# Summing, norming and projecting the tokens of layer 3 inside its first block of queries

## The chip, the core and the metric

The kernel runs on one core of a Trainium2 chip. The core has a matrix engine (TensorE, "PE" in the profile; its weight loads are listed as "PEld"), a vector engine (VectorE, "DVE"), an engine for activation functions (ScalarE, "ACT"), a general engine (GpSimd, "POOL") and a queue for transfers (SyncE, "SP"). Each engine works through its own instructions in order and waits for others by semaphores. Working memory is SBUF, matrix products land in PSUM (eight banks), and everything larger is in DRAM, which transfers (DMA) read and write.

The metric is the time of one execution on the device in microseconds, as a median over several runs; lower is better.

## The reference

A network of four layers on an image of 256 channels and 64 x 64 points, in float32. Layers 0 and 1 work on the image, layers 2 and 3 on its 4096 points as tokens of 256 numbers. Layers 2 and 3 each add an attention to the tokens and then a mixture of eight experts, of which each token uses two. The change lies between the experts of layer 2 and the attention of layer 3:

```python
t = t + _L2_ffn_ref(_ln_t(t), ...)                 # experts of layer 2
t = t + _L3_attn_ref(_ln_t(t), Wq, bq, Wk, bk, Wv, bv)
t = t + _L3_ffn_ref(_ln_t(t), Wg, bg, W1, b1, W2, b2)

def _L3_attn_ref(x, Wq, bq, Wk, bk, Wv, bv):
    Q = x @ Wq + bq; K = x @ Wk + bk; V = x @ Wv + bv
    weights = softmax(Q @ K.T / sqrt(256))         # 4096 x 4096
    return weights @ V
```

`_ln_t` takes each token's mean away and divides by its deviation.

## The kernel before, in words

**Names.** A token tile is 128 tokens (there are 32), a block is four tiles, 512 tokens (eight blocks, `NBLK`, index `b`), a pair is two tiles (16 pairs, `NPAIR`, index `j`). The tokens stay in SBUF as `t`.

**Layer 2's experts** (`experts`, L1844; `expert_tiles`, L1861) read sorted tokens from the DRAM table `xs` and write each token's two outputs to the DRAM table `ys` with scattered transfers (L1925). The table is filled by scatters of layer 2's route (L1784). Between the two, `attn3` has begun: it forms the product of the weights of queries and keys (`wqk`, L2033 to L2037) and the weights of values (`wvp`, L2028) from three matrices that are loaded under the name `weights3` (L2335, L2336). Tiles are allotted from pools that are stacked: a pool opened later lies behind those still open, and a tile that lies in memory of an earlier pool waits until the earlier tile is done with.

**Norm and projection** (L2043 to L2068, called "the stage between" in this document). For each of the eight blocks: `combine` loads the experts' two outputs (`f_g`, 512 KB each, one half issued on SP's queue, one on ScalarE's) and adds them to `t` with two additions on VectorE (L1963). `layer_norm` (L192) takes statistics on VectorE, the root on ScalarE (L204), and applies the norm on ScalarE (L211); the result is written into `vs`, the tile of values. TensorE turns it (L2052), ScalarE copies it to `ks` (L2054), TensorE multiplies it with `wqk` (L146 through `mm`), ScalarE adds the bias (L2060), and the queries go to DRAM (`qd`, L2061). VectorE forms four sums and differences of keys (L2063 to L2066), and the keys go to DRAM (`kd`, L2068). `ks` has two buffers.

**The attention** (L2069 on). All products are made by a scheme with seven products in place of eight on halves of the matrices, which needs sums and differences of the operands. It goes over blocks of queries and within each over pairs of keys; one (block, pair) is a step `g`, 128 steps in all.

- `fetch(g)` (L2086) loads the keys of a pair (`kt`), with the first pair of a block also the queries, of which VectorE makes four differences (L2093 to L2096). In the first block it also takes a maximum over the keys (L2104) and forms four sums and differences of values in place on GpSimd (L2107 to L2110).
- `scores(g)` (L2122) is seven products into three PSUM banks. One bank (`sa`) is written, copied by ScalarE (L2132), added to by VectorE (L2133), and written again within the step. `together` (L2112) combines them with four operations on VectorE, ScalarE takes exponentials (L2144), and VectorE forms their differences `et` with three operations (L2147 to L2149).
- `values(g)` (L2152) is seven products of exponentials with values, summed in four PSUM banks over the pairs of a block.
- `finish` (L2172) multiplies with `wvp`, divides by the sum and adds to `t`, for one tile of the block before; `route` (L1730) norms those tokens, picks the experts and scatters them to `xs`. Its tile of norms `rn` and its turned tile `rT` have one buffer each.

In the loop (L2186) `values` follows `scores` by `LAG` = 1 step. Within `manual_schedule` TensorE's instructions stand in the order in which they are written; on the other engines and queues a planner sets the order, from its own estimate of when each instruction can start, with what is written earlier going first among those that can.

Of the kernel before, what the change touches and what calls it, by code (L numbers as in the profile page):

```python
# [19 lines left out]
P = 128  # L20
# [33 lines left out]
LAG = 1  # L54
# [34 lines left out]
class Net:  # L89
# [1071 lines left out]
    def store(self, t, out, more=False):  # L1161

        with (
# [3 lines left out]
            for b in range(NBLK):  # L1167
                o = pool.tile([P, 2, NB], F32, tag="o", name="st_o")
                y = self.outputs(b, pool) if more else None
# [779 lines left out]
    def outputs(self, b, pool):  # L1949

        y = pool.tile([P, 2, TPB, C], F32, tag="g", name="f_g")
# [5 lines left out]
    def combine(self, b, t, pool):  # L1957

        nc = self.nc
        y = self.outputs(b, pool)  # L1960
        part = t[:, b * TPB : (b + 1) * TPB, :]
        for r in range(2):
            nc.vector.tensor_tensor(part, part, y[:, r], ALU.add)  # L1963
# [43 lines left out]
    def attn3(self, t, S):  # L2007
# [6 lines left out]
        with (  # L2014
# [12 lines left out]
            wvp = w["w_v3p"]  # L2027
            nc.vector.tensor_tensor(wvp, wvp, w["w_v3s"], ALU.subtract)  # L2028
            with tc.tile_pool(name="a3m_ps", bufs=1, space=PSUM) as ps:
# [9 lines left out]
            with (  # L2039
                tc.tile_pool(name="a3n", bufs=2) as wp,  # L2040
                tc.tile_pool(name="a3n_ps", bufs=2, space=PSUM) as ps,
            ):
                for b in range(NBLK):  # L2043
                    self.combine(b, t, wp)
                    n = [vs[:, 2 * b + i // 2, 2 * (i % 2) : 2 * (i % 2) + 2, :].rearrange("p s c -> p (s c)") for i in range(TPB)]
                    self.layer_norm(wp, t[:, b * TPB : (b + 1) * TPB, :], n, 1e-5, on_act=True)

                    ks = wp.tile([P, 2, 8, P], F32, tag="ks", name="a3_ks")
                    for k in range(2):
                        p = ps.tile([P, NB], F32, tag="tr", name="tr_ps")  # L2050
                        for i in range(TPB):
                            nc.tensor.matmul(p[:, i * P : (i + 1) * P], n[i][:, k * P : (k + 1) * P], self.ident, is_transpose=True,  # L2052
                                             start=(i == 0), stop=(i == TPB - 1))
                        nc.scalar.copy(ks[:, :, 2 * k : 2 * k + 2, :], p.rearrange("p (r s n) -> p r s n", r=2, s=2))  # L2054
                    nc.vector.memset(vs[:, 2 * b : 2 * b + 2, 1 : 4 : 2, P - 1 : P], 1.0)
                    qT = wp.tile([P, 2, NB], F32, tag="qT", name="a3_qT")
                    for m in range(2):
# [408 lines left out]
```

## Time and profile before

| what | us |
|---|---|
| median of 5 runs (3776.49 to 3793.88) | 3778.69 |
| the profiled execution | 3789.68 |
| its span, first to last instruction | 3787.8 |
| last scatter of layer 2's experts issued (L1925) | 2256.2 |
| first load of experts' outputs issued (L1954) | 2259.2 |
| first turn (L2052) on TensorE | 2276.1 |
| last projection done on ScalarE (L2060) | 2328.7 |
| first product of scores (L2128) | 2337.1 |
| first product of the second block of queries | 2437.2 |
| last product of values, about | 3171.8 |
| first load of tokens for layer 3's experts (L1875) | 3206.6 |

Over the span TensorE is busy 90%, VectorE 58%, GpSimd 38%, ScalarE 36%. Times inside the execution are counted from the span's start. A row of the order of time gives start, length, engine, line, operation, what is written and read, and in brackets the idle time before it with what ended it. A row of a group gives busy time in all and the mean time of one in ns after the first bar, and the idle time before after the second. TensorE's rows count two instructions for one product in float32.

### The profile page before, as it was taken

The page shows a single profiled execution, that of the slowest core. Times are in us where ns is not written, and L with a number is a line of the kernel's source. Part 1 is how long each engine was busy: PE and PEld are TensorE (multiplying, and loading weights), DVE is VectorE, ACT ScalarE, POOL GpSimd, SP SyncE. Part 2 cuts the span into 40 slices and gives each one's busy share as a digit, 9 for nine tenths or more (in the row PEclk, how much of TensorE's full clock was granted, in tenths as well). Part 3 has the DMA queues.
Part 4 walks back from the last instruction along what each step waited for, and adds up shares of the span by engine and source line. Part 5 has one row for each costly group of instructions (what it writes and reads, how often), then busy time and mean ns, then how long its engine had stood idle before and what let it go on. Part 6 is the DMA issues. An engine that isn't in the chain of part 4 may idle for free. (4 is left out here: it accounts for less than half of the span.)

```text
span 3787.8 us, 59679 instructions
## 1 busy us (share of the span) xinstructions
PE 3415.9 (90%) x22332; PEld 2393.8 (63%) x22332; DVE 2210.8 (58%) x5433; ACT 1360.3 (36%) x2783; POOL 1433.6 (38%) x1416
## 2 busy tenths in 40 slices
PE   6989999999997788986876977999999996999997
PEld 4433334334333688854665754888888885888886
DVE  6756656566565577788554547777777775111111
ACT  5544343343432566432111334222222221333331
POOL 1038888888883455534323333000000001111110
PEclk9999999999998899998785998999999997999999
DMA  1004414301013322200001866232232322555554
GB/s 56 3 28 114 130 56 122 101 24 40 21 40 127 94 68 68 68 18 1 24 33 52 271 216 240 89 101 85 94 100 96 96 95 88 196 200 186 195 189 175
DMA packets 160975, 378.27 MB, mean 100 GB/s; under 512 B 17377, under 2 KB 75490, under 8 KB 151458
## 3 DMA queue, kind: packets, MB, share of 16 engines
q1 hardware_dynamic: 136450, 318.96, 25.7%
q0 software_dynamic: 13056, 35.93, 2.5%
q10 hardware_dynamic: 11168, 19.42, 1.5%
q8 instruction: 182, 2.98, 0.3%
q14 instruction: 119, 0.97, 0.1%
HBM read 273.96 MB, written 100.29 MB: 99 GB/s over the span
## 5 line engine op out<-in xcount | busy, mean ns | idle before, releaser
L583 POOL TENSOR_TENSOR l_sm<-l_sc,mask 128x512 f32<-128x512 f32 (+3 forms) x624 | 770.0, 1270 | 118.8 <-ACT l_sc L573 116.4
L577 DVE TENSOR_TENSOR l_sm<-l_s,mask 128x256 f32<-128x256 f32 (+3 forms) x1248 | 492.1, 447 | 300.6 <-PE l_s L567 290.9
L573 ACT COPY l_sc<-l_s 128x384 f32<-128x384 f32 (+3 forms) x896 | 367.6, 461 | 558.2 <-PE l_s L567 541.4
L567 PE MATMUL l_s<-l_q,l_k 32*128 32x384 f32 (+2 forms) x3584 | 425.6, 515 | 5.6 <-DVE l_sm L577 2.4
L146 PE MATMUL f_h_ps<-f_xT,f_w 128*128 128x256 f32 x1440 | 346.6, 389 | 16.2 <-DVE f_xT L1888 6.5
L1784 POOL DMA_INDIRECT xs<-f_n,f_to x64 | 62.7, 980 | 788.4 <-DVE a_qt L2096 577.1
L1925 POOL DMA_INDIRECT ys<-f_y,f_at x144 | 138.9, 965 | 577.9 <-ACT f_y L1924 530.4
L146 PE MATMUL f_y_ps<-f_w,f_h 128*128 128x256 f32 x1440 | 328.1, 379 | 0.0
L146 PEld LDWEIGHTS f_h_ps<-f_xT,f_w 128*128 128x128 f32 x1440 | 266.4, 192 | 85.8 <-ACT f_h L1898 20.9
L567 PEld LDWEIGHTS l_s<-l_q,l_k 32*128 32x128 f32 x3584 | 165.6, 184 | 241.4 <-issue 125.2
L146 PEld LDWEIGHTS f_y_ps<-f_w,f_h 128*128 128x128 f32 x1440 | 268.2, 190 | 33.7
L2144 ACT ACTIVATE a_e<-a_e 128x512 f32<-128x512 f32 x256 | 156.8, 629 | 241.9 <-DVE a_e L2117 222.8
L952 DVE TENSOR_TENSOR l_pr<-l_vk,l_w_ps 128x1280 f32<-128x1280 f32 x128 | 186.5, 1481 | 55.1 <-PE l_acc_ps L956 37.5
L1898 ACT ACTIVATE f_h<-f_h_ps,f_w 128x256 f32<-128x256 f32 x360 | 163.7, 468 | 134.3 <-PE f_h_ps L146 125.3
L956 PE MATMUL l_acc_ps<-ident,l_pr 128*128 128x128 f32 x1600 | 196.9, 277 | 9.3 <-POOL l_pr L947 9.2
L956 PEld LDWEIGHTS l_acc_ps<-ident,l_pr 128*128 128x128 f32 x1600 | 183.5, 143 | 15.8 <-POOL l_pr L947 10.9
L1924 ACT ACTIVATE f_y<-f_y,f_wgt 128x256 f32<-128x256 f32 x144 | 65.3, 500 | 329.8 <-DVE f_y L1922 296.9
L610 PE MATMUL l_a_ps<-l_sm,l_v 128*32 128x512 f32 (+3 forms) x1408 | 178.7, 530 | 1.9 <-POOL l_sm L583 1.8
L610 PE MATMUL l_b_ps<-l_sm,l_v 128*32 128x256 f32 (+2 forms) x2176 | 171.5, 376 | 0.5 <-POOL l_sm L583 0.5
L2128 PE MATMUL a_sa_ps<-a_q,a_kt 128*128 128x256 f32 x512 | 155.7, 386 | 17.9 <-DMA a_kt<-a_kd 9.1
L2132 ACT COPY a_u<-a_sa_ps 128x256 f32<-128x256 f32 x128 | 47.6, 372 | 328.3 <-PE a_sa_ps L2128 314.6
L1922 DVE TENSOR_TENSOR f_y<-f_y_ps,f_w 128x512 f32<-128x512 f32 x72 | 49.8, 691 | 196.2 <-PE f_y_ps L146 188.5
(500 smaller groups left out, 6318.4 us busy)
## 6 DMA issues: line engine op xcount, KB each, us to landing
a_kt<-a_kd SPq DMA_DIRECT2D x128, 512.0 KB
f_w<-in_f_w SPq DMA_DIRECT2D x36, 1152.0 KB
f_w<-in_f_w SPq DMA_DIRECT2D x36, 1028.0 KB
xs<-zero SPq DMA_DIRECT2D x8, 4160.0 KB
l_vk<-vt SPq DMA_DIRECT2D x180, 128.0 KB
f_x<-xs SPq DMA_DIRECT2D x72, 260.0 KB
f_w<-in_f_w SPq DMA_DIRECT2D x36, 384.0 KB
l_rcp<-l_recd SPq DMA_DIRECT2D x48, 256.0 KB
```

The lines of the kernel that those rows point to most:

```text
L146: self.nc.tensor.matmul(out, lhsT, rhs, start=(i == 0), stop=(i == len(pairs) - 1))
L567: nc.tensor.matmul(s[pair, j], k[hp, key * P : (key + 1) * P], qs[hp], start=True, stop=True)
L573: nc.scalar.copy(sc[:, j], s[1, j])
L577: nc.vector.tensor_tensor(sms[0][:, j, at : at + t * wide].rearrange("p (t n) -> p t n", n=wide), part[:, which, :], mask, ALU.mult)
L583: nc.gpsimd.tensor_tensor(sms[1][:, :, at : at + t * wide].rearrange("p j (t n) -> p j t n", n=wide), part[:, :, which, :], bc(mask, 1, 2) ...
L610: nc.tensor.matmul(out, v[:, key, hp], sms[pair][:, j, base + lo * wide : base + hi * wide], start=not seen[nm], stop=(left[nm] == 0 and h ...
L952: nc.vector.tensor_tensor(pr, vk, bc(held["w"][:, j, dy], 3, D), ALU.mult)
L956: nc.tensor.matmul(acc[:, m, j, :], pf[:, dx, m * P : (m + 1) * P], self.ident, is_transpose=True, start=(j == 0 and dy == 0 and dx == 0 a ...
L1898: nc.scalar.activation(h[:, m, :], q, AF.Gelu, bias=w1[:, 2 * hidden + m : 2 * hidden + m + 1])
L1925: nc.gpsimd.indirect_dma_start(out=self.ys_parts[(i % 4) * NI + k], in_=y[:, k, :], in_offset=None, out_offset=bass.IndirectOffsetOnAxis(a ...
L2128: mm = lambda out, i, right: nc.tensor.matmul(out, A[i], right, start=True, stop=True)
L2144: nc.scalar.activation(e[:, i : i + 3 : 2], e[:, i : i + 3 : 2], AF.Exp, scale=1.0 / 16.0)
```

## The change

The stage between is taken apart into three functions, `norm(b)` (load, sum, norm), `turn(b, k)` (one half of the turn and its copy) and `ask(b, m)` (one half of the projection; with the second half also the writes of queries and keys and the differences of keys). Blocks 0 and 1 are done ahead of the loop. Blocks 2 to 7 are done in steps 0 to 11 of the first block of queries: in an even step the turn, in an odd step the projection, one half between `scores` and `values`, one half after them; `norm` is written one block ahead. `LAG` becomes 2. In the first block of queries `et` is formed on GpSimd, and GpSimd's order, too, is as written. `fetch(g + 3)` is written at the end of a step and no longer at its start.

Memory: the loaded sums, the route's norms and its turned tile share one tile, `room`, with two buffers; `ks` has one buffer; the queries share a tile with the attention's output. `wvp` gets a tile of its own in the pool `a3`, and the pool `weights3` is opened inside `attn3`, behind the pool `a3`, and closed before the experts of layer 2 begin.

```diff
-LAG = 1
+LAG = 2
...
-            wvp = w["w_v3p"]
-            nc.vector.tensor_tensor(wvp, wvp, w["w_v3s"], ALU.subtract)
-            with tc.tile_pool(name="a3m_ps", bufs=1, space=PSUM) as ps:
+            wvp = pool.tile([P, 2, C + 1], F32, tag="wvp", name="a3_wvp")
+            with (
+                tc.tile_pool(name="weights3", bufs=1) as wpool,
+                tc.tile_pool(name="a3m_ps", bufs=1, space=PSUM) as ps,
+            ):
+                self.weights(wpool, ["w_qkT3", "w_v3p", "w_v3s"])
+                nc.vector.tensor_tensor(wvp, w["w_v3p"], w["w_v3s"], ALU.subtract)
...
+                banks = ["q", "sa", "sb", "sc"]
+                kss, qTs = {}, {}
...
+                room = lambda: wp.tile([P, TPB * CX + 2 * NB], F32, tag="room", name="f_room")
+
+                def norm(b):
+
+                    y = room()[:, : 2 * TPB * C].rearrange("p (r i c) -> p r i c", r=2, c=C)
+                    self.outputs(b, y)
+                    part = t[:, b * TPB : (b + 1) * TPB, :]
+                    for r in range(2):
+                        nc.vector.tensor_tensor(part, part, y[:, r], ALU.add)
+                    self.layer_norm(wp, part, [places(b, i) for i in range(TPB)], 1e-5, on_act=True)
...
+                def turn(b, k):
+
+                    if k == 0:
+                        kss[b] = wp.tile([P, 2, 8, P], F32, tag="ks", name="a3_ks", bufs=1)
+                    p = bank()
+                    for i in range(TPB):
+                        nc.tensor.matmul(p[:, i * P : (i + 1) * P], places(b, i)[:, k * P : (k + 1) * P], self.ident, is_transpose=True,
+                                         start=(i == 0), stop=(i == TPB - 1))
+                    nc.scalar.copy(kss[b][:, :, 2 * k : 2 * k + 2, :], p.rearrange("p (r s n) -> p r s n", r=2, s=2))
+
+                def ask(b, m):
+
+                    ks = kss[b]
+                    if m == 0:
+                        nc.vector.memset(vs[:, 2 * b : 2 * b + 2, 1 : 4 : 2, P - 1 : P], 1.0)
+                        qTs[b] = wp.tile([P, 2, NB], F32, tag="oT", name="a3_qT", bufs=1)
+                    p = bank()
+                    self.mm(p, [(wqk[:, kt, m * P : (m + 1) * P], ks[:, :, 2 * kt : 2 * kt + 2, :]) for kt in range(2)])
+                    nc.scalar.activation(qTs[b][:, m, :], p, AF.Identity, bias=bqk[:, m : m + 1])
+                    if m == 1:
+                        nc.sync.dma_start(out=qd[b], in_=qTs[b])
...
                 def route(t0, T):
-                    rn = wp.tile([P, TPB, CX], F32, tag="rn", name="f_n", bufs=1)
-                    rT = wp.tile([P, 2, NB], F32, tag="rT", name="f_nT", bufs=1)
-                    return self.route(t0, T, t, S, wp, rn[:, :T], rT[:, :, : T * P], bank)
+                    r = room()
...
-                    nc.vector.tensor_tensor(et[:, 0:2], e[:, 1:3], e[:, 0:2], ALU.subtract)
+                    eng = nc.gpsimd if b == 0 else nc.vector
+                    eng.tensor_tensor(et[:, 0:2], e[:, 1:3], e[:, 0:2], ALU.subtract)
...
-                with tc.manual_schedule(engines={mybir.EngineType.PE}):
+                with tc.manual_schedule(engines={mybir.EngineType.PE, mybir.EngineType.Pool}):
                     G = NBLK * NPAIR
+                    norm(0)
+                    norm(1)
+                    for b in range(2):
+                        turn(b, 0)
+                        turn(b, 1)
+                        if b == 0:
+                            norm(2)
+                        ask(b, 0)
+                        ask(b, 1)
                     for g in range(3):
                         fetch(g)
+                    banks[:] = ["q"]
                     steps = iter(())
                     for g in range(G + LAG):
+
+                        late = 2 + g // 2
+                        if g % 2 == 0 and late + 1 < NBLK:
+                            norm(late + 1)
+                        if g < G:
+                            scores(g)
+                        if late < NBLK:
+                            (turn, ask)[g % 2](late, 0)
+                        if g >= LAG:
+                            values(g - LAG)
+                        if late < NBLK:
+                            (turn, ask)[g % 2](late, 1)
                         if g + 3 < G:
                             fetch(g + 3)
-                        if g < G:
-                            scores(g)
-                        if g >= LAG:
-                            values(g - LAG)
...
-                    with tc.tile_pool(name="weights3", bufs=1) as wpool:
-                        self.weights(wpool, ["w_qkT3", "w_v3p", "w_v3s"])
-                        self.attn3(t, S)
+                    self.attn3(t, S)
```

## The prediction

> **What bounds the kernel now.** I read the table of stages first, then the order of time around the stage that the change takes apart, then single groups for prices. The chain of waits reaches back only to 3199 us, behind the part in question, so it is of no use here.
>
> ```profile
> core 0: us, PE busy (x) PEld busy (x) DVE busy (x) ACT busy (x) POOL busy (x), PEclk, DMA share, GB/s
> 2256.00:2332.00 76.00, 43.27 (x128) 21.11 (x128) 52.50 (x144) 36.99 (x73) 37.17 (x65) 0.77 0.74 280
> 2332.00:2438.00 106.00, 97.81 (x438) 84.38 (x439) 79.17 (x157) 26.86 (x49) 0.19 (x1) 0.95 0.34 114
> 2438.00:2542.00 104.00, 103.32 (x492) 90.14 (x491) 77.18 (x183) 29.30 (x54) 0.00 (x0) 1.00 0.27 86
> ```
>
> From 2332 on TensorE is full: 103.3 of 104 us in a block of queries, GpSimd next to idle. In the 76 us before it, where the tokens are summed, normed and projected (L2043 to L2068), nothing is full: TensorE 57%, VectorE 69%, DMA 74%. This is what the change folds into the first block of queries.
>
> ```profile
> 2278.71 6.38 PE L146 MATMUL a_q_ps<-a_ks,a_wqk 128*128 128x512 f32 x8 [0.46 <-ACT a_ks L2054]
> 2284.93 1.04 PE L2052 MATMUL tr_ps<-ident,a_vs 128*128 128x128 f32 x8
> 2286.34 3.70 PE L146 MATMUL a_q_ps<-a_ks,a_wqk 128*128 128x512 f32 x8 [0.38 <-ACT a_ks L2054]
> ...
> 2328.73 0.32 SPq L2061 DMA_DIRECT2D a_qd<-a_qT  x1
> 2332.06 0.32 SPq L2091 DMA_DIRECT2D a_q<-a_qd  x1
> 2337.11 1.19 PE L2128 MATMUL a_sa_ps<-a_q,a_kt 128*128 128x256 f32 x2 [9.13 <-DMA a_kt<-a_kd]
> ...
> 2437.23 0.59 PE L2128 MATMUL a_sa_ps<-a_q,a_kt 128*128 128x256 f32 x2
> ```
>
> A block costs TensorE 1.04 us of transposes and eight passes of 0.43 (3.45 us): 4.5 us. A write of queries is read back 3.33 us after its issue (2328.73 to 2332.06), and scoring starts 5.05 us after that. The last line is step 16, the first of the second block of queries. Step 2 starts at 2351.99, so a step takes (2437.23 - 2351.99) / 14 = 6.09 us, of which 14 products of 0.432 are 6.04: no slack.
>
> ```profile
> 2371.24 0.37 ACT L2132 COPY a_u<-a_sa_ps 128x256 f32<-128x256 f32 x1 [2.40 <-PE a_sa_ps L2128]
> 2371.65 0.42 DVE L2133 TENSOR_TENSOR a_u<-a_u,a_sa_ps 128x256 f32<-128x256 f32 x1
> 2372.28 0.59 PE L2128 MATMUL a_sa_ps<-a_q,a_kt 128*128 128x256 f32 x2
> ```
>
> Inside each step TensorE writes a bank (start 2370.12), ScalarE copies it, VectorE adds to it, and five products after the start TensorE writes it again. 2370.12 + 5 x 0.432 = 2372.28: this loop just fits, so whatever stands in front of the copy or the add on its engine is added to the step.
>
> **The change, part by part.** All is reckoned on the profiled execution (3789.68 us, span 3787.8); it lies 11 us above the median of 3778.69, and I subtract the same difference from the median.
>
> *Scoring starts earlier.* Blocks 0 and 1 stay ahead of the loop. Block 0's projection ends, as now, at 2278.71 + 6.38 = 2285.1, its queries are written at 2285.84, read back 3.33 later (2289.2), and 5.05 later scoring starts: 2294.2. On SP's queue the loads of step 0 now stand near three writes of block 1 and loads of sums, and the tile of keys has one buffer instead of two, so I add 1.3: 2295.5, against 2337.1, **-41.6**. Ends: 2291 (block 1's projection ends at 2290.0 and nothing else waits) and 2300 (step 0's loads behind block 1's last write).
>
> *The moved work.* Steps 0 and 1: now 14.9 us (2337.11 to 2351.99); then, without values, 6.9 for step 0 (2337.11 to 2344.01 now) and 3.0 + 3.5 for step 1 with a projection: 13.4, -1.5. Block 2's TensorE work is in it; blocks 3 to 7 add 5 x 4.5 = **+22.5** to steps 2 to 11, which become 8.3 us on average; steps 12 to 15 stay at 6.09. LAG = 2 adds no work: one pair of values is only a step later, and at the end its products follow without a wait.
>
> *Stalls of the loop inside a step.* Prices:
>
> ```profile
> L211 ACT ACTIVATE a_vs<-t,ln_shift,ln_rstd 128x256 f32<-128x256 f32 x32 | 17.1, 596 | 5.1 <-DVE ln_shift L208 5.0
> L1963 DVE TENSOR_TENSOR t<-t,f_g 128x1024 f32<-128x1024 f32 x16 | 20.1, 1260 | 11.3 <-DMA f_g<-ys 11.3
> L2063 DVE TENSOR_TENSOR a_ks<-a_ks 128x256 f32<-128x256 f32 x8 | 5.0, 631 | 0.0
> L2147 DVE TENSOR_TENSOR a_et<-a_e 128x512 f32<-128x512 f32 x14 | 9.7, 692 | 9.7 <-ACT a_e L2144 9.7
> L583 POOL TENSOR_TENSOR l_sm<-l_sc,mask 128x512 f32<-128x512 f32 x240 | 272.4, 1161 | 34.1 <-ACT l_sc L573 34.0 <-POOL l_sm L583 0.2
> L583 POOL TENSOR_TENSOR l_sm<-l_sc,mask 128x256 f32<-128x256 f32 x104 | 70.2, 675 | 0.0
> ```
>
> The three differences leave VectorE (0.69 + 2 x 0.42 = 1.5 us a step) and cost GpSimd 1.16 + 2 x 0.68 = 2.5; with four sums of values (0.53 to 0.66 each) GpSimd works 4.9 of 8.3 us, and its result is due two steps later: no cost on its own. In two steps of together 16.6 us VectorE does sums 2 x 1.26, statistics 4 x (0.40 + 0.16), three small ones 0.56, key differences 2.4, and 2 x 3.3 of the scores with the reduce over keys: some 14.3 us, 86%. ScalarE does exponentials and copies 3.3, norms 4 x 0.60, two copies 1.17, two biased copies 1.37, the root 0.2 and up to two table loads of 1.28 (root, then exponential again): 11 us, 66%. An operation in progress when the loop needs its engine has, on average, a third of a microsecond left (half of the sum of squares over the sum), so 0.27 on VectorE and 0.23 on ScalarE, 0.5, and 0.1 for an order planned with other durations: **0.6 a step, +6** over ten steps. Ends: 0.05, from the later blocks, where VectorE is 75% busy (543.3 of 729 us) and TensorE loses 5.7 us in 112 steps; and 2.5, a whole sum and a whole table load in each.
>
> A row speaks to what GpSimd does to VectorE: a key difference takes 0.41 us at its shortest and 0.63 on average where GpSimd adds values; that is in the 2.4 above. The Trainium skill goes further (SBUF — State Buffer, Who interferes with whom): VectorE and GpSimd share a port pair under an exclusive lock, and the loser is held for the whole of the other's instruction. By that rule the six two-input operations in two steps would each wait behind GpSimd's longer differences; by half of 1.16 us each this would be 3.5 us in two steps or 17 over ten steps, and the total +6 instead of -12.
>
> *Queues.* Six blocks bring their loads and stores into the loop: on SP's queue four issues each (one half of the sums' load, two of keys, one of queries, 0.32 to 0.8 us each) between the loads of keys, on ScalarE's the other half (0.35 each). SP has time: 24 issues, at most 19 us of some 100. Keys are loaded three steps ahead, and a key block is written two steps (16 us) before it is scored, against 3.33 + 5.05 for the round trip: hidden; without that cover each late key block would cost up to 8 us. A load on ScalarE's queue that waits for a free room holds the copies and exponentials behind it; before the loop ScalarE stands 16.4 us behind such loads. There the data are late anyway; in the loop I count it in the upper end of the stalls. GpSimd now runs in written order: a step's differences stand ahead of the sums of values of three steps on, which are read five steps later. The tile of weights copied for itself and the refactored load cost nothing: the same instructions.
>
> *Weights.* The weights of layer 3 are now placed behind the tile of values and norms instead of ahead of it. There the row is:
>
> ```profile
> 2078.63 0.42 DVE L2034 COPY a_wqk<-a_w_ps 128x256 f32<-128x256 f32 x1 [6.15 <-DMA xs<-a_qk,f_to]
> 2080.55 0.40 SPq L1875 DMA_DIRECT2D f_x<-xs  x1
> 2083.92 1.09 PE L1886 MATMUL f_x_ps<-ident,f_x 128*128 128x128 f32 x4 [12.09 <-DVE f_second L1907]
> ```
>
> The copy shares no data with layer 2's scatters; it waits because its tile, 65 KB into the same room, lies in their memory. Weights that lie 61 KB in would wait for the same event, so their loads are issued at 2078.6 instead of 2050.2. About 3.7 us to land (2082.3), 5.3 us of products with them (2066.59 to 2071.83 now, hidden), 2087.6; and the experts' first tokens lie where the weights lay, so their load, 2080.55 now, waits till 2087.8: +7.3 on the whole of layer 2's experts. If only TensorE's order delays them it is 3 or so, if the room lies elsewhere 0. I take **+6**, near the row's end, since the wait above is seen.
>
> *The last route.* It waits for its own single buffer: VectorE sits 3.2 us until the scatters of the route before have left (L213 at 3181.82; the reciprocal it needs is done at 3178.62). The room now has two buffers: **-3.2** (ends -3.2 and 0).
>
> Sum: -41.6 - 1.5 + 22.5 + 6 + 6 - 3.2 = -11.8; 3778 for the execution, **3767** as a median.
>
> **Rivals.** First, *only the gain*: stalls as in the later blocks (0.1), weights in time: -41.6 - 1.5 + 22.5 + 1 - 3.2 = -23, 3756. For it: 5.7 us in 729. Against: ScalarE was 28% busy there. Second, *given back*: 1.2 us of stall and the full 7.3: -4.5, 3774. For it: 1.28 us table loads in front of the copy. Third, *slower*: VectorE becomes the bound in steps 2 to 11, held by GpSimd's longer operations and then behind its own queue, at 11.3 us a step (3 of stall): -41.6 - 1.5 + 22.5 + 30 + 7.3 - 3.2 = +13.5, 3792. It decides from 1.65 us of stall a step on. For it: 86% is close; against: the row's 0.22 a difference. Fourth, *it does not do what it says*: queue order on SP holds step 0's loads behind later blocks' sums, scoring starts at 2310: +3, 3781.
>
> **How the numbers follow.** A measurement of this kernel tells some 0.3% (11 us) from no change. Forecast 0.40 (its own range 3756 to 3774, stalls 0.1 to 1.2 and weights 0 to 7.3), only the gain 0.22, given back 0.20, slower 0.13, late start 0.05. Faster by over 0.3% (below 3767.4): half of the forecast, 0.21, and the first rival, 0.22: 0.43. Slower (above 3790.0): the third rival, 0.13, and 0.04 from the edges of the fourth and of "given back": 0.17. Within: the rest, 0.40. The range leaves out a tenth at each side: 3750 to 3790.
>
> **What would show it.** First score product of layer 3 near 2302 (2295.5 + 6); steps 2 to 11 at 8.9 us, steps 12 to 15 at 6.1; step 16 near 2429; the experts' first transposes near 2090; L213 of the last route without a wait on scatters. The prediction is wrong if those ten steps take over 10 us, if VectorE waits for loads or GpSimd in them, or if the start lies past 2310.

## The result: no gain, and up to a third of a per cent slower

The changed kernel takes 3793.71 us (median of 36 runs, 3782.47 to 3808.54) against 3780.15 of the kernel before (62 runs, 3769.53 to 3795.3): a ratio of 1.0035, 95% interval 1.0027 to 1.0042, or some 13 us more. It was put on a chip twice more: 3785.51 against 3777.35 (1.0023, 1.0005 to 1.0041) and 3758.66 against 3756.23 (1.0005, 0.9996 to 1.0014). So it is a gain on none of them, and how much it loses differs from chip to chip.

The profiled executions don't show the totals: that of the kernel before, 3789.68 us, lies 10 us above its median, that of the changed kernel, 3781.28 us (span 3779.1), 12 below. What differs there is layer 2, whose instructions stand in the same order in both kernels (the last section has numbers). So lengths of stages are compared from here on, from three profiles of each kernel:

| stage | before (us) | after (us) | difference of means |
|---|---|---|---|
| layer 2's last scatter to the experts' first transposes | 7.9, 7.9, 7.9 | 15.9, 15.7, 15.9 | +7.9 |
| layer 2's experts, to their last product | 168.6, 168.2, 164.0 | 166.1, 166.5, 170.1 | +0.6 |
| to layer 3's first transposes | 23.6, 23.9, 23.9 | 23.7, 22.9, 23.7 | -0.4 |
| to the first score product | 61.0, 60.3, 61.5 | 27.2, 27.2, 27.6 | -33.6 |
| steps 0 and 1 | 14.9, 14.8, 14.9 | 15.6, 18.9, 17.0 | +2.3 |
| steps 2 to 11 | 61.1, 60.4, 60.4 | 90.9, 88.6, 90.8 | +29.5 |
| steps 12 to 15 | 24.2, 24.2, 24.2 | 24.8, 25.0, 25.0 | +0.7 |
| step 16 to the last route's last scatter | 766.6, 766.4, 766.4 | 767.4, 767.3, 763.9 | -0.3 |
| to the end | 584.0, 583.8, 584.9 | 581.5, 583.0, 583.4 | -1.6 |

Together +5. The experts and the end run the same code in both kernels and still vary (164 to 170 us and 582 to 585), so this sum is known to a few us only; the rows that the change touches add up to +6. The whole fold, from the first transposes to step 16, took 160.6 us before and takes 159.6 now, and as 3.0 us of values only moved behind step 16, it gains nothing; the placement of the weights costs 7.9. The changed kernel's busy times by window, in the columns of the prediction's table of stages:

```profile
core 0: us, PE busy (x) PEld busy (x) DVE busy (x) ACT busy (x) POOL busy (x), PEclk, DMA share, GB/s
2252.00:2299.00 47.00, 16.88 (x33) 7.49 (x34) 34.61 (x103) 18.06 (x38) 9.74 (x13) 0.60 0.73 256
2299.00:2430.00 131.00, 120.28 (x516) 92.08 (x517) 71.31 (x149) 47.65 (x87) 69.21 (x98) 1.00 0.45 160
2430.00:2535.00 105.00, 103.34 (x489) 90.14 (x488) 77.72 (x180) 29.20 (x54) 2.12 (x4) 1.00 0.27 85
```

The 76 us in which nothing was full have become 47, and they are crowded still: VectorE 74%, DMA 73%. In the first block TensorE works 120 of 131 us, and VectorE, which the prediction saw nearly full there, only 71. The start, in order of time (start, duration, engine, line, tiles, and what ended the wait before it):

```profile
2271.64 2.80 PE L2073 MATMUL a_q_ps<-ident,a_vs 128*128 128x128 f32 x8 [23.73 <-ACT a_vs L211]
...
2277.88 5.49 PE L146 MATMUL a_q_ps<-a_ks,a_wqk 128*128 128x512 f32 x6 [1.54 <-ACT a_ks L2075]
...
2284.11 0.61 SPq L2087 DMA_DIRECT2D a_qd<-a_qT  x1
2288.94 1.86 SPq L2118 DMA_DIRECT2D a_kt<-a_kd  x2
...
2290.84 5.37 PE L146 MATMUL a_q_ps<-a_ks,a_wqk 128*128 128x512 f32 x8 [6.23 <-ACT a_ks L2075]
2291.37 0.32 SPq L2108 DMA_DIRECT2D a_q<-a_qd  x1
2298.86 0.67 PE L2145 MATMUL a_sa_ps<-a_q,a_kt 128*128 128x256 f32 x2 [2.66 <-DMA a_q<-a_qd]
```

Block 0's queries are written at 2284.11, the load that reads them back is issued 7.26 us later (3.33 in the kernel before), and the first product comes 7.49 us after that (5.05 before). Scoring starts 27.2 us after the first transposes, where the prediction had 2295.5 - 2276.1 = 19.4. The other long wait, 6.23 us, is block 1's copy into the one tile of keys, which block 0's writes hold.

What the load waits for last is the write itself: its landing, as the semaphores in the trace give it, comes 7.24 us after its issue (7.24 to 7.68 in the three profiles, 3.24 to 3.25 in those of the kernel before). The two loads of keys (2288.94) stand ahead of it in SP's queue, but they had been issued by 2290.8, half a microsecond before the write landed at 2291.35. The two halves of the round trip, in the kernel before and in the changed one:

```profile
2328.73:2332.06 3.33, 0.00 (x0) 0.00 (x0) 0.00 (x0) 0.00 (x0) 0.00 (x0) 0.98 0.82 327
2332.06:2337.11 5.05, 0.01 (x1) 0.04 (x1) 1.61 (x5) 0.00 (x0) 0.19 (x1) 0.50 0.81 278
```

```profile
2284.11:2291.37 7.26, 1.03 (x6) 0.76 (x5) 5.48 (x16) 3.32 (x8) 2.62 (x4) 0.73 0.96 327
2291.37:2298.86 7.49, 4.83 (x8) 1.61 (x7) 5.09 (x21) 4.14 (x10) 0.00 (x0) 0.81 0.98 355
```

The DMA engines were 82% busy during the round trip before and are 96 to 98% busy now, when the loads of the sums run too.

The weights:

```profile
2068.92 0.37 SPq L124 DMA_DIRECT2D w_qkT<-in_w_qkT  x1
...
2073.79 2.05 PE L146 MATMUL a_w_ps<-w_qkT 128*128 128x256 f32 x4 [17.89 <-DMA w_v3s<-in_w_v3s]
...
2078.19 0.85 PE L146 MATMUL a_b_ps<-pp,w_qkT 128*128 128x1 f32 x4
2079.07 0.40 SPq L1875 DMA_DIRECT2D f_x<-xs  x1
2081.83 1.09 PE L1886 MATMUL f_x_ps<-ident,f_x 128*128 128x128 f32 x4 [2.79 <-DMA f_x<-xs]
```

Their loads are issued at 2068.92, after layer 2's last scatter (issued at 2065.9), TensorE stands 17.89 us until they have landed, and the load of the experts' first tokens leaves (2079.07) when their last product ends (2079.04), as the prediction had it.

### The profile page after: what moved, and what is told of

Read it like the earlier page. It is cut to its first block, busy times and chain, and to the rows that moved or that the text cites. A ratio compares the mean times of both kernels' runs of the same rounds, so it can differ in the third digit from the quotient of the medians.

```text
span 3779.1 us, 59700 instructions
## 1 busy us (share of the span) xinstructions
PE 3414.8 (90%) x22332; PEld 2386.4 (63%) x22332; DVE 2186.9 (58%) x5385; ACT 1362.5 (36%) x2785; POOL 1481.0 (39%) x1464
## 5 line engine op out<-in xcount | busy, mean ns | idle before, releaser
L1784 POOL DMA_INDIRECT xs<-f_room,f_to x64 | 64.1, 1001 | 700.5 <-issue 587.9
L146 PEld LDWEIGHTS f_h_ps<-f_xT,f_w 128*128 128x128 f32 x1440 | 265.7, 192 | 83.0 <-ACT f_h L1898 18.9
L1898 ACT ACTIVATE f_h<-f_h_ps,f_w 128x256 f32<-128x256 f32 x360 | 164.0, 469 | 137.4 <-PE f_h_ps L146 134.5
L956 PEld LDWEIGHTS l_acc_ps<-ident,l_pr 128*128 128x128 f32 x1600 | 184.1, 143 | 14.5 <-POOL l_pr L947 9.6
```

The lines of the kernel that those rows point to most:

```text
L146: self.nc.tensor.matmul(out, lhsT, rhs, start=(i == 0), stop=(i == len(pairs) - 1))
L956: nc.tensor.matmul(acc[:, m, j, :], pf[:, dx, m * P : (m + 1) * P], self.ident, is_transpose=True, start=(j == 0 and dy == 0 and dx == 0 a ...
L1898: nc.scalar.activation(h[:, m, :], q, AF.Gelu, bias=w1[:, 2 * hidden + m : 2 * hidden + m + 1])
```

## The experiments

Each was timed against the kernel before on its own chip; ratios are to that. Stage lengths are from the profile of each.

### The weights' place, undone in the changed kernel and done alone in the kernel before

```diff
-                tc.tile_pool(name="weights3", bufs=1) as wpool,
                 tc.tile_pool(name="a3m_ps", bufs=1, space=PSUM) as ps,
             ):
-                self.weights(wpool, ["w_qkT3", "w_v3p", "w_v3s"])
...
-                    self.attn3(t, S)
+                    with tc.tile_pool(name="weights3", bufs=1) as wpool:
+                        self.weights(wpool, ["w_qkT3", "w_v3p", "w_v3s"])
+                        self.attn3(t, S)
```

> The changed kernel with layer 3's weights opened ahead of the tile of values, as before; nothing else. Placement theory: the wait of their loads on layer 2's scatters goes, last scatter to the experts' first transposes falls from 15.9 to 8 us, and the time by 8 us, 3786. Rival (the wait is hidden by the experts' own loads, and what costs the time is in the first block): no change, 3794.

Measured: 3779.86 us, ratio 0.9998 (0.9982 to 1.0013), where the unaltered changed kernel had 1.0023 on the same chip. Last scatter to first transposes: 8.1 us.

```profile
2036.01 0.37 SPq L124 DMA_DIRECT2D w_qkT<-in_w_qkT  x1
...
2052.11 2.05 PE L146 MATMUL a_w_ps<-w_qkT 128*128 128x256 f32 x4 [0.51 <-PE f_r_ps L146]
...
2069.67 1.09 PE L1886 MATMUL f_x_ps<-ident,f_x 128*128 128x128 f32 x4 [12.31 <-DVE f_second L1907]
```

The loads leave 26 us before layer 2's last scatter (2061.6) instead of 3 us after it, the products stand beside layer 2's last route, and the experts' first transposes follow their own tokens. (The row names `f_second`; VectorE forms it as soon as those tokens have landed.) The same edit the other way round, the kernel before with only the weights moved behind the tile of values:

> The kernel before with the one placement moved: layer 3's weights opened behind the tile of values, their difference in a tile of its own; no step is folded. Placement theory: last layer 2 scatter to the experts' first transposes grows from 7.9 to 15.8 us and the time by 8 us, 3786 to 3787, which is the larger part of what the change lost. Rival (the 8 us are lost only together with the rest of the change): under 3 us, 3780.

Measured: 3788.98 us, ratio 1.0019 (1.0003 to 1.0034), some 6 to 7 us; last scatter to first transposes 15.6 us, and the later stages as in the kernel before. The same wait shows, in a kernel that folds nothing:

```profile
2067.55 2.05 PE L146 MATMUL a_w_ps<-w_qkT 128*128 128x256 f32 x4 [17.59 <-DMA w_v3s<-in_w_v3s]
...
2075.54 1.09 PE L1886 MATMUL f_x_ps<-ident,f_x 128*128 128x128 f32 x4 [2.74 <-DMA f_x<-xs]
```

The placement costs 7.6 to 7.8 us of that stage by itself (6 to 9 by the times), nothing hides it, and it belongs to no other part of the change.

### The late start: a second tile of keys

```diff
-                        kss[b] = wp.tile([P, 2, 8, P], F32, tag="ks", name="a3_ks", bufs=1)
+                        kss[b] = wp.tile([P, 2, 8, P], F32, tag="ks", name="a3_ks")
```

> The changed kernel with two tiles of keys instead of one (the queries' tile stays single); nothing else. Late-start theory: block 1's transposes no longer wait 6.2 us for block 0's key writes, scoring starts 6 us sooner after the first transposes (21 us instead of 27.2), the time falls by 6 us, 3788. Rival (the wait moves to the queries' tile or to SP's queue): the start gains under 2 us, 3793. If GpSimd holding VectorE were what costs the time, neither this nor the weights would matter.

Measured: 3789.48 us, ratio 1.0024 (1.0008 to 1.0041): no gain. My theory fell. Block 1's wait did go, and scoring started later, 29.7 us after the first transposes:

```profile
2288.14 3.70 PE L146 MATMUL a_q_ps<-a_ks,a_wqk 128*128 128x512 f32 x8 [0.38 <-ACT a_ks L2075]
2305.98 1.19 PE L2145 MATMUL a_sa_ps<-a_q,a_kt 128*128 128x256 f32 x2 [14.14 <-DMA a_q<-a_qd]
...
2297.51 0.32 SPq L2087 DMA_DIRECT2D a_qd<-a_qT  x1
2297.88 0.85 SPq L2094 DMA_DIRECT2D a_kd<-a_ks  x1
2298.79 0.84 SPq L2108 DMA_DIRECT2D a_q<-a_qd  x1
```

TensorE runs straight on and then stands 14.14 us for block 0's queries: their load now sits in SP's queue behind block 1's writes (2297.51). Block 1's queries go into the one tile that block 0's write reads, and that write, issued at 2288.51, landed at 2296.12, so block 1's write and the load behind it came after that. The 6.23 us had been in the shadow of the round trip.

### The late start: no round trip

```diff
                     if m == 0:
...
+                        if b == 0:
+                            qTs[b] = wp.tile([P, 2, NB], F32, tag="q", name="a3_q")
+                        else:
+                            qTs[b] = wp.tile([P, 2, NB], F32, tag="oT", name="a3_qT", bufs=1)
...
                             nc.sync.dma_start(out=kd[2 * b + r], in_=ks[:, r])
+                            if b == 0:
+                                kts[r] = wp.tile([P, 8, P], F32, tag="kt", name="a3_kt", bufs=4)
+                                nc.gpsimd.tensor_copy(kts[r], ks[:, r])
```

In addition the tile of keys has two buffers, block 0's queries are neither written nor loaded (`fetch` takes them as they are), and steps 0 and 1 load no keys.

> The changed kernel with two tiles of keys, block 0's queries written straight into the tile they are scored from, and its two pairs of keys copied on GpSimd instead of being read back; the weights stay where the change put them. If the late start is the round trip of block 0's queries and keys through memory (7.3 us from the write's issue to the load's, then 7.5 to the first product), scoring starts 20 us after the first transposes instead of 27.2 (29.7 with two tiles and the round trip), and the time falls by 7 us against the changed kernel, to 3780 to 3785. If it is TensorE's half clock or VectorE's queue that holds the start, it stays past 25 us and the time with it.

Measured: 3776.95 us, ratio 0.9991 (0.9978 to 1.0004). Scoring starts 15.5 us after the first transposes.

```profile
2283.70 3.70 PE L146 MATMUL a_q_ps<-a_ks,a_wqk 128*128 128x512 f32 x8 [0.38 <-ACT a_ks L2075]
2287.24 0.59 PE L2158 MATMUL a_sa_ps<-a_q,a_kt 128*128 128x256 f32 x2
...
2293.62 0.70 PE L2158 MATMUL a_sa_ps<-a_q,a_kt 128*128 128x256 f32 x2 [3.89 <-DVE a_u L2163]
```

Scores follow block 1's projection without a wait. So the round trip held the start; without it, neither the clock nor VectorE's queue keeps the scores from following the projection. Part is given back at once: in step 0 TensorE stands 3.89 us for VectorE's addition, steps 0 and 1 take 19.6 us, and of the 12 to 14 us won at the start 8 are left at step 16 (151.4 us from the first transposes against 159.6).

### Both mended

Both edits above together; `wvp` is formed in place again (`wvp = w["w_v3p"]`), as before the change, to make room for the second tile of keys.

> The changed kernel with both mended: weights opened ahead of the tile of values (their difference formed in place, as before), and block 0 scored without the round trip, two tiles of keys. If the two losses are separate, they add up: 8 and 7 us below the changed kernel, 3771 to 3775, 5 us below the kernel before. If they overlap, 3778.

Measured: 3766.85 us, ratio 0.9976 (0.996 to 0.9991); start 14.5 us after the first transposes, last scatter to the experts' transposes 7.8. By the stages the losses are separate and add up: 7.9 us at the weights and 7.3 from the first transposes to step 16 (152.3 against 159.6). By the ratio it lies 9 us below the kernel before, where 5 were expected. A second time:

> The kernel with both losses mended, a second time (weights ahead of the tile of values; block 0 scored without the round trip, two tiles of keys): ratio 0.9976 the first time, 0.996 to 0.9991. If it beats the kernel before, 0.997 to 0.998 again, and 12 us below the changed kernel of the same chip; if the first was luck, 1.000.

Measured: 3744.22 us, ratio 0.997 (0.9959 to 0.9981), 14 us below the changed kernel on that chip. So this version was faster than the kernel before on both chips, by 0.2 to 0.3%, and the stages show where.

### GpSimd's share, taken back

```diff
-                    eng = nc.gpsimd if b == 0 else nc.vector
+                    eng = nc.vector
```

> The changed kernel with the exponentials' differences of the first block back on VectorE; nothing else. In the changed kernel's profile VectorE's operations last 3.7 us longer in steps 2 to 11 than the same operations elsewhere, the key differences above all (0.75 instead of 0.42 us), while GpSimd works. If GpSimd holding VectorE is what costs steps 2 to 11 their 9 us instead of 8.3, they shorten to 8.5 or less and the time falls by 4 us or more, to 3780 to 3786. If GpSimd's help is worth its price, VectorE has 15 us more to do in ten steps, they take 9.3 or more and the time rises to 3790 or more.

Measured: 3755.19 us, ratio 1.0012 (1.0003 to 1.002); steps 2 to 11 take 89.6 us, against 88.6 to 90.9. Neither theory's number came: by the steps the edit is worth nothing either way. (The changed kernel itself wasn't timed on this chip.) GpSimd keeps its sums of values here, so only its differences are tested. What GpSimd does to VectorE is seen all the same. One of the four key operations (min, median and max in ns, eight of them each), in the changed kernel and then with the differences on VectorE:

```profile
L2089 DVE TENSOR_TENSOR a_ks<-a_ks x8: 389/834/1118, 2279.9 to 2396.1; 128x256 f32<-128x256 f32 x8
```

```profile
L2089 DVE TENSOR_TENSOR a_ks<-a_ks x8: 387/425/497, 2258.7 to 2375.7; 128x256 f32<-128x256 f32 x8
```

This one takes twice as long with GpSimd's differences beside it; the other three have the same medians in both kernels (0.56, 0.42 and 0.48 us). But VectorE has slack there: its instructions in steps 2 to 11 add up to some 51 of 90.9 us, and to 65 of 89.6 with the differences its own. So neither the longer operations nor the 15 us of moved work reach TensorE.

### VectorE in the written order

```diff
-                with tc.manual_schedule(engines={mybir.EngineType.PE, mybir.EngineType.Pool}):
+                with tc.manual_schedule(engines={mybir.EngineType.PE, mybir.EngineType.Pool, mybir.EngineType.DVE}):
...
-                        if g % 2 == 0 and late + 1 < NBLK:
-                            norm(late + 1)
                         if g < G:
                             scores(g)
+                        if g % 2 == 0 and late + 1 < NBLK:
+                            norm(late + 1)
```

> The changed kernel with VectorE, too, in the written order, and a step's sums written behind its scores. In the changed kernel seven of eight blocks' sums (L2062) run before the first score product, though six of them are written into the steps: VectorE is in the planner's order. If this crowd in front is what makes the start late, the first score product comes 22 us after the first transposes instead of 27.2, VectorE's work in steps 2 to 11 grows from 51 to 75 us and the steps take 9.5 us or more; the time then stays within 5 us of the changed kernel. If VectorE's order is not what holds the start, it stays at 27, and later sums only add: 3800 or more.

Measured: 3850.36 us, ratio 1.0263 (1.0247 to 1.028). The order of the sums (L2062: count; min, median, max in ns; first and last start), in the changed kernel and in this one, whose scores start at 2262.4:

```profile
L2062 DVE TENSOR_TENSOR t<-t,f_room x16: 1191/1225/1743, 2259.3 to 2314.1; 128x1024 f32<-128x1024 f32 x16
```

```profile
L2062 DVE TENSOR_TENSOR t<-t,f_room x16: 1217/1224/1226, 2232.9 to 2357.5; 128x1024 f32<-128x1024 f32 x16
```

In the changed kernel 14 of 16 sums start by 2290.4, before the first score product at 2298.86, and the last two in step 1. Five blocks' sums (3 to 7; not six, as the expectation has it) are written into steps 0 to 8, and four of the five are summed in front of the loop, because only TensorE and GpSimd keep the written order. In order, the sums reach to 2357.5, well into the steps; the first transposes come 18.7 us after the last expert product instead of 23.7, and scoring starts 23.3 us after them instead of 27.2. So the crowd does hold the start, by 9 us in all, 4 of them after the first transposes. But steps 2 to 11 take 106.9 us, TensorE waits 16.1 us in them for VectorE (whose work there is 65 us, not the 75 expected), the second block takes 114.8 us instead of 105.0, and from step 63 to the last scatter it is 50 us more: the planner's order is better than the written one in the later blocks. The time was to stay within 5 us of the changed kernel; this size was far outside what I expected. The version with both losses mended did no better in that order:

> The kernel with both losses mended, with VectorE in the written order as well. Without the round trip the start came 14.5 us after the first transposes, and steps 0 and 1 took 20.8 us, 5.4 of them TensorE's wait for VectorE's addition (L2150 of the changed kernel), which stood behind sums and reductions. If the planner's order in front of those two steps is the cause, they shorten by 4 to 6 us and the time to some 3762; if the written order costs the steps more than that, the time is 3770 or more.

Measured: 3840.31 us, ratio 1.0236 (1.0223 to 1.025); steps 0 and 1 took 29.2 us, 11.0 of them TensorE's wait for that addition where 5.4 had been. So the written order costs those steps more, the second of the two cases, by far more than the number that I put to it. With the written order up to the first loads of keys alone:

```diff
+                with tc.manual_schedule(engines={mybir.EngineType.PE, mybir.EngineType.Pool, mybir.EngineType.DVE}):
                     G = NBLK * NPAIR
...
                     for g in range(3):
                         fetch(g)
+                with tc.manual_schedule(engines={mybir.EngineType.PE, mybir.EngineType.Pool}):
                     banks[:] = ["q"]
```

> Both losses mended, and VectorE in the written order up to the first loads of keys alone, in the planner's order behind. In the fully ordered one the first transposes came 17.6 us after the last expert product instead of 22.9, the first score product 33.3 us after it instead of 37.4; its steps were the slow part. If the crowd of sums in front is what still costs, the start gains 4 us and the steps stay as they are in the mended kernel (20.8 and 92.2 us): 0.9965. If the sums that leave the front only come back in steps 0 to 3, the ratio is that of the mended kernel or higher.

Measured: 3743.39 us, ratio 0.9961 (0.9948 to 0.9975), beside 3744.22 of the mended kernel on the same chip: inconclusive. The first transposes come 16.9 us after the last expert product instead of 23.2, but GpSimd's copies of keys then hold the first product 7.8 us, steps 2 to 11 grow from 92.1 to 95.0 us, and step 16 lies 176.5 us after the last expert product where it lay at 175.7. What leaves the front comes back in the steps.

### Values two steps late, alone

The kernel before with `LAG = 2`.

> The kernel before with values two steps behind the scores instead of one; nothing else. My sum took 3.0 us for a pair's values out of the first two steps and put them nowhere. If they only move to the end of the loop, step 16 starts 3.0 us sooner after step 0 (97 us instead of 100.2), the stretch from step 16 to the last route's last scatter grows by 3.0 us (766.6 to 769.6), and the time stays at 3778. If the longer lag frees the loop, it falls by 3 us; if it makes it wait for tiles, it rises.

Measured: 3770.79 us, ratio 0.9981 (0.9964 to 0.9997), while the stages of its profile showed no gain. So again:

> The kernel before with values two steps behind the scores, a second time: the first time the median lay 7 us below the kernel before (ratio 0.9981, 0.9964 to 0.9997), while its profile showed 99.9 us for steps 0 to 15 (100.2 before) and 768.2 from step 16 to the last scatter (766.6), no gain. If the profile is right, the ratio is 1.000; if the gain is real, 0.998 again.

Measured: 3753.48 us, ratio 1.0003 (0.9993 to 1.0013): no effect. The first result did not come again. Of the 3.0 us one part of the expectation came and the other didn't: the time from the last score product to the last product of values grows from 6.5 to 9.5 us in both profiles, but steps 0 to 15 take 99.9 and 102.0 us instead of 97. Steps 0 and 1 get 1.5 us shorter, not 3.0 (13.4 for 14.9), and steps 2 to 11 take 62.3 and 64.4 us where they took 60.4 to 61.1. TensorE waits 1.9 to 2.6 us there for VectorE; in the second profile its granted clock was 0.96 instead of 1.00 as well.

### The two kernels again

> The changed kernel unaltered, for a second profile and times beside its variants. Two profiles of one kernel each so far: layer 2's sum stage (L1439, first to last) took 239.0 us in the kernel before and 225.7 in the changed one, though its code is the same. If that is noise, this profile shows something between 222 and 245, the time is some 3794 us and the ratio 1.0035, with +8 us at the weights (last layer 2 scatter to the experts' first transposes 15.9 us). If the change does something to layer 2, 225.7 comes again.

Measured: 3785.51 us, ratio 1.0023 (1.0005 to 1.0041); layer 2's sum stage 222.5 us, weights 15.7. The stages came as expected; the ratio was to be 1.0035.

> The kernel before unaltered, for a second profile: ratio 1.000. Last layer 2 scatter to the experts' first transposes 7.9 us, last expert product to step 16 184.7 us, last scatter to the end 584 us, each within 2 us. If layer 2's sum stage is noise, it is some 225 to 240 us here; if it belongs to the program, 239.

Measured: 3778.25 us, ratio 0.9993 (0.9977 to 1.0009); that stage 234.5 us, the others within 2 us as expected.

> The changed kernel unaltered, a third time. By the stages of the profiles so far the change costs some 4 us (weights +8, first block and tail together -1, the experts -2, the end -1), by the times 13.5 and then 8 to 9. If the stages tell the truth and layer 2's sum stage (201 to 239 us in kernels that share its code) makes the rest, the ratio is 1.001 to 1.0025 where that stage is steady; if something is lost that the stages don't show, 1.0035 again.

Measured: 3758.66 us, ratio 1.0005 (0.9996 to 1.0014); the sum stage 204.0 us.

> The kernel before unaltered, a third time, to pair with the changed kernel on one chip: ratio 1.000, and from layer 2's last scatter to the end 1710 to 1712 us, against 1713 to 1715 of the changed kernel.

Measured: 3751.96 us, ratio 0.9988 (0.9979 to 0.9997); the sum stage 202.0 us. The changed kernel lies 6.7 us above this run and 2.4 above all runs of the kernel before on that chip; from layer 2's last scatter to the end it takes 1717.5 us against 1708.1, both outside the ranges expected. Of these 9.4 us, 6.1 are the experts' stage, whose code is the same. The sum of the stages, +5, lies between the two differences of the times; on this chip nothing is lost that the stages don't show. The kernel before, timed against itself, gave 0.9988 with an interval that leaves out 1, so a ratio within 0.2% tells little by itself, and the readings here rest on the stages.

## Why the prediction was wrong

The forecast was 3767, 12 us faster; the stages say 5 slower, the times 2 to 13. Of the prediction's own signs of being wrong, the start lies before 2310 and the ten steps take 9 us; only VectorE's wait for loads came, and it cost little. What failed is the sum, above all the price of the round trip in front of the loop. The working, step by step:

- **Scoring starts earlier: -41.6, measured -33.6.** This is the largest error, 8 us. The sum took the write at 9.7 us after the first transposes, 3.33 to the load and 5.05 to the product from the end of the stage between, and added 1.3 for the queue. Measured are 12.5, 7.26 and 7.49. The write came late because ScalarE did block 1's norms ahead of the second copy of block 0's turned tokens (L2075), for which TensorE stood 1.54 us, and because the projection's rows add up to 7.57 us (2.08 and 5.49) where they had taken 6.38. The load was issued as soon as the write had landed, and that took 7.24 us instead of 3.24. The order of SP's queue, for which the 1.3 was added, came second: the loads of keys ahead of this one waited for the keys' writes in their turn, and would have held it until 2290.9 by themselves. That the round trip is what held the start is shown by the version without it (15.5 us). Why it takes longer is likely the loads of the sums beside it (DMA share 0.96 to 0.98 instead of 0.82); no run takes these away alone. The single tile of keys, the other reason named for the 1.3, was not the cause.
- **Steps 0 and 1: -1.5, measured +2.3.** Step 1 was put at 6.5 us and takes 10.0 in the first profile: TensorE waits 2.2 us there for the addition (L2150), behind a key difference of 1.12 us and a reduce over keys, and 0.8 for ScalarE's biased copy. The sum had these two steps run without a stall; it counted stalls from step 2 on. The other two profiles show the same waits but 18.9 and 17.0 us for the two steps in place of 15.6: there the granted clock was 0.82 and 0.90 instead of 1.00 (0.83 to 0.86 in the kernel before), and TensorE was busy 14.8 and 13.0 us instead of 11.5. So part of the +2.3 is the clock's.

```profile
2306.85 1.12 DVE L2089 TENSOR_TENSOR a_ks<-a_ks 128x256 f32<-128x256 f32 x1 [0.42 <-ACT a_ks L2075]
2307.89 0.67 DVE L2121 TENSOR_REDUCE f_big<-a_kt 128x2 f32<-128x512 f32 x1
2308.49 0.41 DVE L2150 TENSOR_TENSOR a_u<-a_u,a_sa_ps 128x256 f32<-128x256 f32 x1
...
2308.94 0.70 PE L2145 MATMUL a_sa_ps<-a_q,a_kt 128*128 128x256 f32 x2 [2.19 <-DVE a_u L2150]
```

- **"LAG = 2 adds no work: one pair of values is only a step later": +3.0, put at nothing.** The sum dropped a pair's values from step 1 and added them nowhere. In the changed kernel 196 of TensorE's instructions for values lie before step 16, 210 in the kernel before (two make one product, so a pair's seven products are missing), and the end of the loop is 3.0 us longer (6.5 to 9.5 us). This was an error of bookkeeping, and it could have been seen without a run.
- **Blocks 3 to 7's TensorE work, +22.5, and 0.6 us of stall a step, +6: right in number, the second by luck.** Steps 2 to 11 take 8.9 to 9.1 us (8.9 forecast); TensorE is busy 24 us longer in them and waits 3.8 to 6.2 us, all for L2150. The ground given was wrong: VectorE was to be 86% busy with sums and norms in the steps, and its instructions add up to 56%, because the planner had done most of them before. Most sums had not moved where the diff writes them. They still crowd the start, which is where the prediction should have charged them (9 us in the version with VectorE in order). What stands in front of the addition instead is, in the first profile, statistics in step 2 (1.8 us of TensorE's 6.2), key differences in the odd steps (0.3 each), and in steps 4, 6 and 10 the reduce over keys (2.7 in all), which waits for the keys' load. The prediction had these loads hidden: VectorE waits 30 us for them in the ten steps, 4 before. Step 10:

```profile
2388.09 0.69 DVE L2121 TENSOR_REDUCE f_big<-a_kt 128x2 f32<-128x512 f32 x1 [6.31 <-DMA a_kt<-a_kd]
2389.36 0.69 DVE L2121 TENSOR_REDUCE f_big<-a_kt 128x2 f32<-128x512 f32 x1 [0.59 <-DMA a_kt<-a_kd]
2389.97 0.41 DVE L2150 TENSOR_TENSOR a_u<-a_u,a_sa_ps 128x256 f32<-128x256 f32 x1
2390.43 0.48 PE L2145 MATMUL a_sa_ps<-a_q,a_kt 128*128 128x256 f32 x1 [1.31 <-DVE a_u L2150]
```

- **Weights: +6, measured +7.9.** Right in mechanism; the row's own +7.3 was the better value. Two experiments show it alone.
- **The last route: -3.2, measured -2.9.** Right: without the wait its norm (L213) follows at once, and from the reciprocal ahead of it (L205) to the last scatter it takes 22.5 us instead of 25.4. The norm before, then now:

```profile
3181.82 1.38 DVE L213 TENSOR_SCALAR f_n<-t,ln_mv,ln_rstd 128x256 f32<-128x256 f32 x4 [3.21 <-DMA xs<-f_n,f_to]
```

```profile
3175.46 1.50 DVE L213 TENSOR_SCALAR f_room<-t,ln_mv,ln_rstd 128x256 f32<-128x256 f32 x4 [0.23 <-issue]
```

With the measured terms (-33.6 + 2.3 + 29.5 + 0.7 + 7.9 + 3.0 - 2.9) the same sum gives +6.9, near the +6 of the rows that the change touches.

Of the rivals, "slower" named the right sign by a mechanism that did not act: VectorE held by GpSimd until the steps reach 11.3 us. The Trainium skill (SBUF — State Buffer, Who interferes with whom) states that the two share ports under a lock. The trace agrees in so far as an operation of VectorE takes longer beside GpSimd's (834 against 425 ns at the median for one of the four key operations), and no run here shows a cost in time from it, since VectorE has slack. That the prediction's +6 by that rule lies near the measured time is chance. "Late start" was the nearest in cause, but it had scoring at 2310 because SP's order holds the loads back; the start came 8 us late, at 27.2 instead of 19.4 us after the first transposes, because the writes land late, and only with steps 0 and 1, the weights and the values added did it turn the sign.

Open: the 13 us of the first comparison against 5 in the stages. On the chip where layer 2's sum stage took nearly the same in both kernels (202.0 and 204.0 us) the times agree with the stages; that its changing length makes the rest is likely and wasn't shown. In the two profiles of the first comparison it was 239.0 us before and 225.7 after, the other way round.

## What to carry to other kernels

Price a round trip through memory where it will run, beside the transfers that will run there, and not where it ran before; where the data are on the chip already, score the first block from them. Code written into a loop's steps is there only on engines that keep the written order: look first which engines the planner is free to reorder, and charge the crowd where it will put it. When a tile's room moves, look who held that memory before, and when a step is lagged, find its work again at the end.

## What the runs showed of the hardware

Layer 2's sum stage, the same instructions in the same order in every kernel here, took 201 to 239 us. TensorE is 78 to 87% busy there, and its granted clock alternates between full and half in spells of 3.4 us and its multiples: 113 us at half clock in the 239 us of the first profile of the kernel before, 68 in the 202 of its third, on a chip on which the whole kernel ran some 25 us faster. Ahead of that stage, one and the same product (of `wg_bd`, near 1727 us) took 0.28 us in the first profile of the kernel before and 0.42 in its third, where it fell into a spell of half clock. So executions differ by 10 us and more in a stage that no change touches. The Trainium skill (TensorE: Matmul & The Clock Gate, Part 1: The HAM clock gate) tells of a free-running window of about 3.4 us by whose activity the clock is set; the lengths of the spells agree with it.

A write of one block's queries landed 3.24 us after its issue where the DMA engines were 82% busy, and 7.24 us after it where they were 96% busy, at the same 327 GB/s. What else was under way is the likely reason; no run separates it.

GpSimd's wide difference takes 1.26 us at its shortest, 1.27 at the median and 2.12 at its longest in the changed kernel, a key difference on VectorE 0.39 and 1.12. That the two slow each other, and not GpSimd VectorE alone, is the likely reading; no run separates it.
